# One turn in twelve units: first layers and sums grouped by three pairs in a graph layer on one core

## The chip, the core and the metric

The kernel runs on one core of a Trainium2 chip. The core has a matrix engine (TensorE, PE in the profile, with its weight loads as a row of their own, PEld), a vector engine (VectorE, DVE), a scalar engine (ScalarE, ACT), a general engine (GpSimd, POOL) and a queue engine (SyncE, SP). Each of them takes its own instructions in order, and they wait for one another by semaphores. Matrix results land in PSUM, which has eight banks of 2 KB a partition; everything else lies in SBUF. The metric is the time of one execution on the device, in microseconds (us). The time before is a median of 2561.25 us in three runs (2556.93 to 2567.58).

## The reference

One message-passing layer over 6250 nodes of 256 features and 206250 edges, sorted by target node. For every edge an embedding is made by three matrices, gated by a number of the edge, added to the row of the source node, clipped at zero, and summed by target; the sums go through a small network with a layer norm.

```python
h = relu(layernorm(x))
polarity = clip(edge_attr[:, 0:1], 0, 1);  raw = edge_attr[:, 1:]        # 64 features
e = relu(raw @ W_e1.T + b_e1) @ W_e2.T + b_e2
edge_emb = (e * (polarity + 0.01)) @ W_le.T + b_le
msg = relu(h[src] + edge_emb)
aggr = segment_sum(msg, dst)
t = (h + aggr) @ W_g1.T + b_g1
out = x + relu(layernorm(t) * ln_g + ln_b) @ W_g2.T + b_g2
```

All of it is in 32-bit floats. The kernel multiplies W_e2 and W_le together once, so that an edge needs two layers only. Each 32-bit matmul in the program stands as two matmuls in the profile.

## The kernel before

**Units, blocks and pairs.** The edges are cut into 806 units of 256 edges, two units to a block, two blocks to a pair: 202 pairs, four units each. Six blocks make a group, whose target nodes lie close together, so that its sums fit in 128 rows.

**The work of a unit.** `edge_part(u)` (L264 to L280) does the second layer: 8 matmuls in the profile (L272) into one PSUM bank, which DVE empties into a tile `msg` (L277). `gather` (L527) issues on POOL two gathers for the unit (L537), each bringing 128 rows of `hb_d` from memory into a tile `hg`. Some units later, `whole(u)` (L578) scales `msg` by the gate and adds it to the gathered rows on DVE (L584, two instructions), and ACT clips at zero (L589). How many units later is set by the loop: `LEAD - u // SHRINK`, from 22 units at the start down to 1 at the end.

**The work of a pair.** `first_layer(q)` (L238) makes the first layer of both blocks of a pair: 8 matmuls in the profile (L248) into four PSUM banks, three of which ACT empties (L257) and one DVE (L254). `add_pairs` (L622) sums the finished units of a pair by 16 matmuls in the profile (L601) with 0/1 matrices `sel`, into a bank of its own (`pd`). After the sums of a pair its `hg` tiles are free for later gathers. After the last block of a group `keep` (L606) copies the sums to SBUF on ACT (L613).

**Turns.** The first layers and the sums are issued together, in `turn_of(q)`, behind the second unit of a pair (`u % 4 == TURN`). In the first six and the last six pairs there is a turn in every pair: one first layer, the sums, one raw load. Between them (`by_two`) there is a turn in every second pair, so one in 8 units: the first layer of pair q+2, the sums of all pairs that are finished (two as a rule), the first layer of pair q+3, and two loads of raw features on SP (L235).

**What sets the order.** The instructions stand in the order in which the Python code issues them; no scheduler moves them. PSUM tiles `pz` rotate over seven banks, which second layers, first layers and node work share. In the main loop `forward(u)` comes first, then one small `piece()` of DVE work, then `whole` of the units that are due, then one step of node work (`due`). Two details belong to the turns: in the unit ahead of a turn one `whole` is held back (`made` is kept one lower), and no step of node work is issued in the unit ahead of a turn and in the turn (`now % 8 in QUIET`).

**Pacing of the gathers.** `in_step(us, behind)` (L546) is called behind each second layer, first layer and sum with an estimate of its PE time (1.754 us for a second layer, `EDGE`). It adds this to `spent` and issues gathers while `got * STEP < spent + AFLOAT` (1.282 us a gather, 6 us ahead), each batch behind the matmul named, and never more than the ring of `hg` tiles holds: `2 * (4 * summed + HG)`, with HG = 16 units. From unit 782 on, `gathers(4 * summed + HG)` issues without this pacing whatever the ring has room for.

Of the kernel before, what the change touches and what calls it, by code (L numbers as in the profile page):

```python
# [36 lines left out]
NP = -(-NB // 2)  # L37
MARGIN = 768
DEG = E // N
LEAD = 22  # L40
LEAST = 1
# [1 line left out]
STEP = 1.282  # L43
AFLOAT = 6.0
SHRINK = 36
HG = 16
FEW = 6
QUIET = (0, 1)
TURN = 1
CH = 4  # L50
AHEAD = 10
assert DEG * N == E and NF * GE + S * P >= E
# [21 lines left out]
def chunks():  # L74

    t = 0
    while t < NW:
        n = min(CH, N // P - t)
        if n <= 0:
# [17 lines left out]
def gnn_kernel(ctx: ExitStack, tc: tile.TileContext, x, src_c, dst_c, dst_r, pol_c, raw_t, w_e1t, w_e2,  # L97
               w_let, w_g1t, w_g2t, vec_c, row_v, x_t, out):
    nc = tc.nc
# [117 lines left out]
    with fast:  # L217
# [11 lines left out]
        def ps():  # L229
            return psz.tile([P, 2, D], F32, name="pz")  # L230

        def load_pair(q):
            if q < NP:
                raw[q] = ld.tile([P, 512], F32, name="raw")
                nc.sync.dma_start(out=raw[q], in_=raw_t[q])  # L235

        def first_layer(q):

            bs = [b for b in (2 * q, 2 * q + 1) if b < NB]
            if not bs:  # L240
                return
            for b in bs:
                e1[b] = e1_p.tile([P, 2, 512], F32, name="e1")
            pe = {}
            for c in range(2):
                for s, b in enumerate(bs):
                    pe[s, c] = ps().rearrange("p a b -> p (a b)")
                    z = nc.tensor.matmul(pe[s, c], we1_s[s * F:(s + 1) * F, c * P:(c + 1) * P],  # L248
                                         raw[q][s * F:(s + 1) * F, :], start=True, stop=True)
                paced(LAYER, z)  # L250
            for c in range(2):
                for s, b in enumerate(bs):
                    if s == c == 1:
                        nc.vector.tensor_scalar(e1[b][:, c, :], pe[s, c], be1_s[:, c:c + 1], 0.0, op0=ALU.add,  # L254
                                                op1=ALU.max)
                    else:
                        nc.scalar.activation(e1[b][:, c, :], pe[s, c], AF.Relu, bias=be1_s[:, c:c + 1])  # L257
            raw.pop(q)
# [5 lines left out]
        def edge_part(u):  # L264

            nonlocal last_z
            b, v = divmod(u, 2)
            pz = ps()
            for i in range(2):
                k = (2 * v + i) * P  # L270
                for c in range(2):
                    last_z = nc.tensor.matmul(pz[:, i, :], e1[b][:, c, k:k + P], wc_s[:, c, :], start=c == 0, stop=c == 1)  # L272
            msg[u] = msg_p.tile([P, 2, D], F32, name="msg")
            if plain(u):
                nc.scalar.activation(msg[u], pz, AF.Copy)
            else:
                nc.vector.tensor_add(msg[u], pz, bc_s)  # L277
            if v == 1:
                e1.pop(b)
            paced(EDGE, last_z)  # L280

        last_z = None
        sums = lambda last: None
        paced = lambda us, behind: None

        def by_two(q):
            return FEW <= q < NP - FEW

        def turn_of(q):


            if not by_two(q):
                if q + 2 < NP:
                    first_layer(q + 2)
                sums(q == NP - 1)
                load_pair(q + 4)
            elif q % 2 == 0:
                first_layer(q + 2)
                sums(False)
                first_layer(q + 3)  # L300
                load_pair(q + 4)
                load_pair(q + 5)

        def forward(u):

            edge_part(u)
            if u % 4 == TURN:
                turn_of(u // 4)
# [33 lines left out]
        with tc.tile_pool(name="p1", bufs=4) as p1, tc.tile_pool(name="p1x", bufs=11) as p1x:  # L342
# [4 lines left out]
            def load_rows(k, halves=1):  # L347
                if k < len(parts):
                    t0, p, t = parts[k]
                    xts[k] = p1x.tile([P, CH, D], F32, name="xt")  # L350
                    h = t // halves
# [4 lines left out]
            def stats(k, i0, i1):  # L356
                t0, p, t = parts[k]
                if i0 == 0:
                    mvs[k] = p1.tile([P, CH, 2], F32, name="mvx")
                for i in range(i0, min(i1, t)):  # L360
                    row_stats(p1, p, 1, lambda _: xts[k][:p, i, :], mvs[k][:, i:i + 1, :])

            def root(k):
                t0, p, t = parts[k]
                nc.scalar.activation(rs_s[:p, t0:t0 + t], mvs[k][:p, :t, 1], AF.Sqrt, bias=eps_t[:p])

            def nodes_out(k):
# [6 lines left out]
                for i in range(t):  # L374
                    nc.scalar.activation(xt[:p, i, :], xt[:p, i, :], AF.Relu, bias=nm_s[:p, t0 + i:t0 + i + 1],
                                         scale=rs_s[:p, t0 + i:t0 + i + 1])
                hb = p1.tile([P, CH, D], F32, name="hb")
                for i in range(t):
# [40 lines left out]
            for k in range(len(parts) + 1):  # L419
# [9 lines left out]
                if k < len(parts):  # L429
                    stats(k, 2, CH)  # L430
                    root(k)
# [3 lines left out]
                for _ in range((k > 0) + (k > 2 and k % 3 > 0)):  # L435
                    u = next(units, None)
# [84 lines left out]

        with tc.tile_pool(name="hg", bufs=HG) as hg_p, tc.tile_pool(name="ms", bufs=5) as ms_p, \
                tc.tile_pool(name="sel2", bufs=9) as sel2_p, tc.tile_pool(name="nd", bufs=3) as nd:
            got = 0
            acc = {}
            made = 0
# [17 lines left out]
            def gathers(last):  # L544

                while got < 2 * min(NU, last):  # L546
                    gather()

            def in_step(us, behind):

                nonlocal spent
                spent += us
                while got * STEP < spent + AFLOAT and got < 2 * min(NU, 4 * summed + HG):
                    gather(behind)
# [16 lines left out]
            def piece():  # L571

                if steps and steps[0][0] <= now:
                    steps.popleft()[1]()
                elif rest:
                    rest.popleft()[1]()
# [63 lines left out]
            now = 0  # L640
# [89 lines left out]
            def due():  # L730

                nonlocal spent
                fns = todo.pop(now, deque())
                if fns and not (by_two(now // 4) and now % 8 in QUIET):
                    spent += NODES
                    fns.popleft()()
                if fns:
                    todo.setdefault(now + 1, deque()).extendleft(reversed(fns))
# [11 lines left out]
            for u in range(LEAD, NU):  # L750
                now = u
                forward(u)

                if u >= NU - 24:
                    gathers(4 * summed + HG)

                piece()
                while made < u + 1 - max(LEAST, LEAD - u // SHRINK) - (by_two(u // 4) and (u + 1) % 8 == TURN):
                    gathers(made + 1)
                    whole(made)  # L760
                    made += 1
                due()
                if len(rest) > 6:
                    piece()
                if u == NU - 24:
                    for w in range(NW):
                        if groups_of(w)[-1] == NG - 1:
                            late[w] = node_work(w, True)
                if u == LEAD + 60:
                    flag = nc.values_load(bad_i[0:1, 0:1], min_val=0, max_val=3 * P)  # L770
            while todo:
                now = min(todo)
# [197 lines left out]
```

## Time and profile before

| | before |
|---|---|
| median of three runs | 2561.25 us (2556.93 to 2567.58) |
| the profiled execution | 2558.52 us, its span 2556.8 us |
| granted TensorE clock, mean | 0.965 |
| PE busy | 2378.9 us, 93% of the span |
| DVE / ACT / POOL busy | 1647.0 / 980.9 / 1638.7 us |
| second layers (L272) on PE | 1486.5 us busy, 51.8 us idle before |
| first layers (L248) on PE | 510.3 us busy, 42.8 us idle before |
| sums (L601) on PE | 258.6 us busy, 53.1 us idle before |
| gathers (L537) on POOL | 1612 of 993 ns |

The span is the time from the first to the last instruction on the core. PE's matmuls overlap and their ends are modelled, so a PE that is shown busy isn't always working at its full rate: the duration of a whole block of matmuls tells more than the busy share. In the chain of waits a row gives a start, a duration and what ran; in the groups a row gives line, engine, operation, tiles and count, then busy time and the mean of one, then the idle time of the engine just before and what ended it.

### The profile page before, as it was taken

The numbers are of one execution on the slowest core, as the hardware profiler recorded it, in microseconds if no ns is written. First come the engines' busy times: TensorE is split into PE (matmuls) and PEld (weight loads), VectorE is DVE, ScalarE is ACT, GpSimd is POOL, SyncE is SP. The second block draws the span as 40 slices with busy tenths as digits, with TensorE's granted clock in tenths as the row PEclk, the third lists the DMA queues.
The fourth block names the chain that finished last, engine by engine and source line by source line (L and its number), as shares of the span: only waits on it lengthen the run. The fifth ranks groups of instructions, "written<-read, shape, count | busy, mean of one in ns | idle before, by whom it ended". The sixth has DMA issues, their size and how long they took to land.

```text
span 2556.8 us, 35901 instructions
## 1 busy us (share of the span) xinstructions
PE 2378.9 (93%) x12382; PEld 1670.3 (65%) x12382; DVE 1647.0 (64%) x3953; ACT 980.9 (38%) x1701; POOL 1638.7 (64%) x1675
## 2 busy tenths in 40 slices
PE   9998998999999989999999999999999999899987
PEld 7666666666666757666666666666666666666664
DVE  7776666666666666666656666656666666656655
ACT  7333333343343433334333433433333433333432
POOL 5666666666666666666666666666666665666662
PEclk9999999999999999998999999999999999999998
DMA  8433343334334433433343444334334333343341
GB/s 300 129 115 113 108 134 112 114 114 130 113 108 125 130 119 106 133 108 117 111 144 101 115 126 122 110 106 137 112 114 131 118 107 114 109 131 109 119 119 55
DMA packets 156084, 309.24 MB, mean 121 GB/s; under 512 B 33183, under 2 KB 77944, under 8 KB 155896
## 3 DMA queue, kind: packets, MB, share of 16 engines
q0 software_dynamic: 77376, 211.39, 28.5%
q1 hardware_dynamic: 77364, 92.23, 11.4%
q10 hardware_dynamic: 1156, 3.28, 0.3%
q8 instruction: 98, 1.61, 0.3%
q14 instruction: 90, 0.74, 0.1%
HBM read 293.92 MB, written 12.85 MB: 120 GB/s over the span
## 4 chain that ended last, share of the span: by engine, by line
PE 82%; issue 5%; DVE 5%; another core or an unknown queue 3%; ACT 1%; DVEq 0%; ACTq 0%
PE pz L272 49%; PE pz L248 17%; PE pd L601 9%; PE pz L701 3%; DVE hg L584 2%; PE pz L195 2%; PE pz L169 2%; DVE msg L277 1%; ACT e L257 0%; DVE sel L566 0%; PE pz L185 0%; ACT hg L589 0%; DVE hT L676 0%; DVE e L254 0%
## 5 line engine op out<-in xcount | busy, mean ns | idle before, releaser
L537 POOL DMA_INDIRECT hg<-hb_d,src_s x1612 | 1601.5, 993 | 861.2 <-issue 525.4
L272 PE MATMUL pz<-wc_s,e 128*128 128x256 f32 x6448 | 1486.5, 384 | 51.8 <-issue 38.6
L272 PEld LDWEIGHTS pz<-wc_s,e 128*128 128x128 f32 x6448 | 1216.7, 192 | 318.8 <-issue 99.8
L589 ACT ACTIVATE hg<-hg 128x512 f32<-128x512 f32 x805 | 508.5, 632 | 1117.2 <-DVE hg L584 854.1
L277 DVE TENSOR_TENSOR msg<-pz,bc_s 128x512 f32<-128x512 f32 x799 | 546.6, 686 | 325.1 <-PE pz L272 152.3
L584 DVE SCALAR_TENSOR_TENSOR hg<-msg,pol_s,hg 128x256 f32<-128x256 f32 x1612 | 697.5, 480 | 2.6 <-issue 1.5
L248 PE MATMUL pz<-raw,we_s 64*128 64x512 f32 x1612 | 510.3, 653 | 42.8 <-issue 22.9
L254 DVE TENSOR_SCALAR e<-pz,vecs 128x512 f32<-128x512 f32 x201 | 150.5, 749 | 500.0 <-PE pz L248 201.4
L257 ACT ACTIVATE e<-pz,vecs 128x512 f32<-128x512 f32 x605 | 376.4, 686 | 225.1 <-PE pz L248 84.9
L248 PEld LDWEIGHTS pz<-raw,we_s 64*128 64x128 f32 x1612 | 177.2, 195 | 281.6 <-issue 164.7
L601 PE MATMUL pd<-hg,sel 128*32 128x256 f32 x3216 | 258.6, 408 | 53.1 <-issue 50.9
L601 PEld LDWEIGHTS pd<-hg,sel 128*32 128x32 f32 x3216 | 114.0, 115 | 221.2 <-issue 170.0
L566 DVE SCALAR_TENSOR_TENSOR sel<-iota_w,zero_c,rel 128x128 f32<-128x128 f32 x403 | 138.8, 344 | 0.0
L613 ACT ACTIVATE ms<-pd 128x256 f32<-128x256 f32 x66 | 25.5, 386 | 191.7 <-remote 60.1
L701 PEld LDWEIGHTS pz<-s,ms 128*128 128x128 f32 x548 | 70.3, 194 | 9.1 <-issue 3.8
L701 PE MATMUL pz<-s,ms 128*128 128x128 f32 x548 | 71.7, 278 | 4.7 <-issue 2.5
L676 DVE SCALAR_TENSOR_TENSOR hT<-hT,zero_c,stb 128x128 f32<-128x128 f32 (+1 forms) x196 | 67.2, 343 | 1.7 <-issue 1.7
L169 PE MATMUL pz<-wg_s,hT 128*128 128x256 f32 (+1 forms) x196 | 52.8, 389 | 9.9 <-DVE hT L703 7.4
L195 PE MATMUL pz<-wg_s,nT 128*128 128x256 f32 (+1 forms) x196 | 53.9, 393 | 5.6 <-ACT hg L589 2.7
L169 PEld LDWEIGHTS pz<-wg_s,hT 128*128 128x128 f32 (+1 forms) x196 | 36.5, 191 | 20.0 <-DVE hT L703 9.7
L379 POOL TENSOR_TENSOR hb<-xt,rows_b 128x256 f32<-128x256 f32 (+1 forms) x49 | 34.2, 729 | 23.4 <-DMA xt<-in_x_dram 12.7
L195 PEld LDWEIGHTS pz<-wg_s,nT 128*128 128x128 f32 (+1 forms) x196 | 37.7, 195 | 15.2 <-issue 6.4
(91 smaller groups left out, 393.0 us busy)
## 6 DMA issues: line engine op xcount, KB each, us to landing
raw<-in_raw_t_dram SPq DMA_DIRECT2D x202, 256.0 KB
hg<-hb_d,src_s POOLq DMA_INDIRECT x1612
stb<-st_d SPq DMA_DIRECT2D x49, 128.0 KB
hb_d<-hb SPq DMA_DIRECT2D x12, 512.0 KB
xt<-in_x_dram SPq DMA_DIRECT2D x48, 128.0 KB
hT<-in_x_t_dram SPq DMA_DIRECT2D x48, 128.0 KB
out_dram<-ot SPq DMA_DIRECT2D x48, 128.0 KB
xt<-in_x_dram SPq DMA_DIRECT2D x11, 512.0 KB
```

The lines of the kernel that those rows point to most:

```text
L169: nc.tensor.matmul(ph[:n, 0, :], aT[:, c, :n], wg1_s[:, c, :], start=c == 0 and not bias_by_pe, stop=c == 1)
L195: nc.tensor.matmul(po[:n, 0, :], nT[:, c, :n], wg2_s[:, c, :], start=c == 0, stop=c == 1)
L248: z = nc.tensor.matmul(pe[s, c], we1_s[s * F:(s + 1) * F, c * P:(c + 1) * P], raw[q][s * F:(s + 1) * F, :], start=True, stop=True)
L254: nc.vector.tensor_scalar(e1[b][:, c, :], pe[s, c], be1_s[:, c:c + 1], 0.0, op0=ALU.add, op1=ALU.max)
L257: nc.scalar.activation(e1[b][:, c, :], pe[s, c], AF.Relu, bias=be1_s[:, c:c + 1])
L272: last_z = nc.tensor.matmul(pz[:, i, :], e1[b][:, c, k:k + P], wc_s[:, c, :], start=c == 0, stop=c == 1)
L277: nc.vector.tensor_add(msg[u], pz, bc_s)
L537: g = nc.gpsimd.indirect_dma_start(out=hg[u][:, i, :], out_offset=None, in_=hb_d, in_offset=bass.IndirectOffsetOnAxis(ap=src_s[:, 2 * u + ...
L584: nc.vector.scalar_tensor_tensor(hg[u][:, i, :], m[:, i, :], pol_s[:, 2 * u + i:2 * u + i + 1], hg[u][:, i, :], op0=ALU.mult, op1=ALU.add)
L589: nc.scalar.activation(hg[u], hg[u], AF.Relu)
L601: z = nc.tensor.matmul(acc[g][j * W:(j + 1) * W, :], sel[g][:, k * S + j, :], m[:, j % 2, :], start=k == 0, stop=b == blocks_of(g)[-1])
L701: nc.tensor.matmul(pa[:, c, :n], ms[g][:, c * P:(c + 1) * P], box["sel2"][i][:, :n], start=i == 0, stop=i == len(gs) - 1)
```

## The change

Between the first six and the last six pairs there is now a turn in every third pair, one in 12 units: the first layer of pair q+1, the sums of all finished pairs (three as a rule), then the first layers of pairs q+2 and q+3 with nothing between them, and three raw loads. `at_turn(u)` names the turns, and the two details (one `whole` held back ahead of a turn, no node step in the turn and ahead of it) follow it. Since `hg` tiles are freed only by the sums, the ring grows from 16 to 20 units. [...]

```diff
-HG = 16
+HG = 20
 FEW = 6
-QUIET = (0, 1)
 TURN = 1
+SET = 3
...
-        def by_two(q):
+        def in_sets(q):
             return FEW <= q < NP - FEW
 
+        def at_turn(u):
+            q, v = divmod(u, 4)
+            return v == TURN and in_sets(q) and (q - FEW) % SET == 1
+
+        def layers_to(q):
+            nonlocal laid
+            while laid <= min(q, NP - 1):
+                first_layer(laid)
+                laid += 1
+
+        def loads_to(q):
+            nonlocal loaded
+            while loaded <= q:
+                load_pair(loaded)
+                loaded += 1
+
         def turn_of(q):
-            if not by_two(q):
-                if q + 2 < NP:
-                    first_layer(q + 2)
+            if not in_sets(q):
+                layers_to(q + 2)
                 sums(q == NP - 1)
-                load_pair(q + 4)
-            elif q % 2 == 0:
-                first_layer(q + 2)
+                loads_to(q + 4)
+            elif at_turn(4 * q + TURN):
+                layers_to(q + 1)
                 sums(False)
-                first_layer(q + 3)
-                load_pair(q + 4)
-                load_pair(q + 5)
+                layers_to(q + SET)
+                loads_to(q + 2 * SET)
+            elif q == FEW:
+                loads_to(q + SET + 1)
...
-                if fns and not (by_two(now // 4) and now % 8 in QUIET):
+                if fns and not (at_turn(now) or at_turn(now + 1)):
...
-                while made < u + 1 - max(LEAST, LEAD - u // SHRINK) - (by_two(u // 4) and (u + 1) % 8 == TURN):
+                while made < u + 1 - max(LEAST, LEAD - u // SHRINK) - at_turn(u + 1):
...
-    nc = bacc.Bacc("TRN2", target_bir_lowering=False, num_devices=1)
+    nc = bacc.Bacc("TRN2", target_bir_lowering=False, num_devices=1, dynamic_dma_scratch_size=8192)
```

1 line of the change is left out of this document (added).

## The prediction

> **What bounds the kernel now.** I read the page first, then the chain of waits over single turns, then the waits of PE, and last the timeline of POOL. On the page PE is busy nearly all the time, so the time is PE's, and three lines make up most of it.
>
> ```profile
> span 2556.8 us, 35901 instructions
> PE 2378.9 (93%) x12382; PEld 1670.3 (65%) x12382; DVE 1647.0 (64%) x3953; ACT 980.9 (38%) x1701; POOL 1638.7 (64%) x1675
> ...
> L537 POOL DMA_INDIRECT hg<-hb_d,src_s x1612 | 1601.5, 993 | 861.2 <-issue 525.4
> L272 PE MATMUL pz<-wc_s,e 128*128 128x256 f32 x6448 | 1486.5, 384 | 51.8 <-issue 38.6
> ...
> L584 DVE SCALAR_TENSOR_TENSOR hg<-msg,pol_s,hg 128x256 f32<-128x256 f32 x1612 | 697.5, 480 | 2.6 <-issue 1.5
> L248 PE MATMUL pz<-raw,we_s 64*128 64x512 f32 x1612 | 510.3, 653 | 42.8 <-issue 22.9
> ...
> L257 ACT ACTIVATE e<-pz,vecs 128x512 f32<-128x512 f32 x605 | 376.4, 686 | 225.1 <-PE pz L248 84.9
> ...
> L601 PE MATMUL pd<-hg,sel 128*32 128x256 f32 x3216 | 258.6, 408 | 53.1 <-issue 50.9
> ```
>
> The chain shows what these cost when nothing disturbs them: first a stretch of second layers and a turn of two pairs, then sums of three pairs, which already occur here and there.
>
> ```profile
> 1198.26 5.18 PE pz L272 x24
> 1203.44 1.92 PE pz L248 x8
> 1205.36 1.86 PE pd L601 x32
> 1207.22 1.92 PE pz L248 x8
> 1209.14 3.65 PE pz L272 x16
> ```
>
> ```profile
> 2163.93 2.73 PE pd L601 x48
> 2166.66 1.92 PE pz L248 x8
> ```
>
> A first layer is 1.92 us, the sums of two pairs 1.86 us, of three 2.73 us: 0.87 us a pair and 0.12 us for the switch. A second-layer matmul in a stretch takes 5.18 / 24 = 0.216 us; 16 of them behind a turn take 3.65 us, 0.20 us over 16 x 0.216.
>
> Now compare with the groups. First layers take 510.3 + 42.8 = 553 us for 202 pairs, clean they would be 202 x 1.92 = 388: 165 us over. Sums take 258.6 + 53.1 = 312 us, clean 202 x 0.87 + 101 x 0.12 = 188: 124 us over. So about 289 us, 2.9 us in each of some 101 turns, are lost in turns; second layers lose little, with 51.8 us idle. What these 289 us are decides the case. The view of line L248 names, for one part, who ended the wait (us, times):
>
> ```profile
>   DVE msg L277: 75.7, 103
>   DVE hg L584: 22.0, 50
>   DVE e L254: 15.0, 22
> ```
>
> Some 113 us of waiting of first layers for DVE: PSUM banks that DVE hasn't emptied yet. The other part, some 176 us, is named "issue". It looks like this (columns of the last fence: stretch, its length, busy us and count of PE, PEld, DVE, ACT and POOL, clock, DMA):
>
> ```profile
> 952.70 0.36 issue
> 953.07 0.38 PE pd L601
> 953.44 1.08 issue
> 954.52 0.59 PE pd L601 x2
> 955.11 0.82 issue
> 955.94 0.38 PE pd L601
> ```
>
> ```profile
> 1203.30:1209.20 5.90, 5.90 (x50) 2.44 (x50) 1.83 (x4) 3.02 (x6) 2.91 (x4) 1.00 0.22 67
> 951.10:960.20 9.10, 4.68 (x35) 1.86 (x33) 3.45 (x8) 2.70 (x4) 5.55 (x6) 0.81 0.34 101
> ```
>
> In the clean turn PE does first layer, sums and first layer in 5.9 us, and POOL issues 4 gathers with a pause. In the slow one the sums alone take 9.1 us: PE gets one matmul about every 0.7 us, while POOL issues gather after gather (here 6). The largest such place is near the end:
>
> ```profile
> 2480.58 0.95 POOL L537 DMA_INDIRECT hg<-hb_d,src_s  x1 [0.30 <-issue]
> ...
> 2499.38 0.95 POOL L537 DMA_INDIRECT hg<-hb_d,src_s  x1 [0.30 <-issue]
> 2508.29 0.95 POOL L537 DMA_INDIRECT hg<-hb_d,src_s  x1 [7.96 <-ACT e L257]
> ```
>
> ```profile
> 2489.70 0.69 DVE L277 TENSOR_TENSOR msg<-pz,bc_s 128x512 f32<-128x512 f32 x1 [8.21 <-remote]
> 2502.36 0.69 DVE L277 TENSOR_TENSOR msg<-pz,bc_s 128x512 f32<-128x512 f32 x1 [10.91 <-remote]
> ```
>
> From 2480.58 to 2499.38 POOL issues 16 gathers, 1.25 us apart, without a pause (the batch that unit 785 issues unpaced). In that time DVE stands still for 8.21 and 10.91 us with no releaser known, and moves on 2 us after the last gather's end. So I read "issue" as what a long unbroken run of gathers does to the other engines. Why it does, the trace doesn't say.
>
> [...]
>
> **The change part by part.**
>
> *Switches between kinds of matmul.* In the pairs 6 to 195 there were 95 turns, now 63. Two first layers in a row occur in the trace:
>
> ```profile
> 72.74 3.87 PE L248 MATMUL pz<-raw,we_s 64*128 64x512 f32 x16
> 76.54 0.70 PE L272 MATMUL pz<-wc_s,e 128*128 128x256 f32 x2
> ```
>
> From start to start 3.80 us, and not held up by the seven banks. Six pairs before: 3 x (1.92 + 1.86 + 1.92 + 0.20) = 17.70 us. After: 2 x (1.92 + 2.73 + 3.80 + 0.20) = 17.30 us. That is 0.40 us in six pairs, and 190 / 6 x 0.40 = **12.7 us less**. No matmul goes away; this is PE's own time and lies on the path wherever the turn is clean.
>
> *Stalls in turns.* 95 of the turns at 2.9 us are 275 us. With 63 turns and a stall f times as long each, they are 183 f. If a turn keeps its stall (f = 1), that is 92 us less. If the stall follows the work in a turn (f = 1.5), nothing changes. If the longer stretch makes it worse, f = 1.8 (the upper end I allow, midway between the mean of 2.9 us and the excess of the slow turn above, 9.1 - 1.86 = 7.2 us) adds 54 us. I take it by parts. The 176 us go with gathers, whose number doesn't change, so 1.5. The 113 us for banks lie between: DVE's backlog builds up over 12 units and not over 8, but the two first layers at the end now come 0.87 us later behind the first one, and node steps are spread over 10 of 12 units and not 6 of 8, so 1.25. The mean is (176 x 1.5 + 113 x 1.25) / 289 = 1.40: **19 us less**.
>
> *The ring.* Room left just ahead of the sums is what it was: 20 - 12 is 16 - 8. Pacing is by PE time, so the ring binds more rarely. At unit 785 it costs: the sums there free the ring, the unpaced line fills it at once, and its reach is four units longer, so the batch is 24 gathers for 16. With DVE stopped as in the rows above, 8 more at 1.25 us are **10 us more**. Bounds: 0, if the longer stop only moves the others' work, and 20 if the stop grows faster than the run.
>
> [...]
>
> *At nothing.* Three raw loads in a turn for two: the number of loads is the same, and the third waits on SP until the first layer of q+2 has read its tile, some 6.6 us into the turn. Behind it on SP stand node loads and stores, and what these bring is used at least three units later, 3 x 1.73 us and the rest of the turn; if that cover went, DVE would wait in `ready`. On ACT the three evictions of a first layer (0.69 us each) fit within the next one's 1.9 us. The held-back `whole` (2 x 0.48 us on DVE) and the quiet units become rarer by a third, worth nothing while DVE waits for PE in turns.
>
> [...]
>
> [...]
>
> The sum: -12.7 - 19 + 10 = about -22 us. The profiled execution took 2558.5 us, 2.7 us below the median. The new median is then 2561 - 22 = **2539 us**, 0.9% less.
>
> **Rivals.**
>
> *The stall belongs to the turn.* f = 1 to 1.2: each turn loses its 2.9 us, however much it holds. For it: DVE's backlog is limited by the seven banks, so it can't grow by half. Against: the slow issue. Time at f = 1.1: -12.7 - 74 + 10, 2484 us.
>
> *Slower: runs of gathers go unbroken.* In a stretch of second layers PE releases 1.754 / 1.282 = 1.37 gathers a unit, 1.71 us of POOL in 1.73 us of PE, so POOL hardly pauses; it is turns that break the run, and they come every 24 gathers, not 16. If runs are stopped by the freeze and not by a turn, DVE, PE and then the clock (0.81 in the slow turn above) pay each time. At f = 1.8: -12.7 + 54 + 10, 2612 us. From f = 1.52 on it is slower than before. [...]
>
> *Nothing is won.* The gathers alone are 1612 x 1.25 = 2015 us of POOL, so whatever PE saves packs them closer and comes back as freezes: f = 1.5, 2558 us.
>
> **How the numbers follow.** About 0.5%, 12.8 us, can be told from no change. My forecast (f from 1.25 to 1.5) has 0.42, the stall of the turn 0.14, unbroken runs 0.32, nothing won 0.12. The first is faster by over 12.8 us for f below 1.45, three quarters of it: 0.31, and with the second 0.45 for faster. The rest of the first and most of the fourth is 0.20 for same; 0.35 for slower. The forecast's own range is 2515 to 2560 us. The range takes half of the second (f = 1.1) and the slower case up to f = 1.75: 2485 to 2603 us.
>
> **What would show it.** Right: in the chain, clean turns of 1.92, 2.73 and 3.80 us; L601's idle and busy sum near 300 us, L248's near 520; DVE's waits before L248 below 100 us in all; a stop of DVE near the end that is 10 us longer, with 24 gathers in a run from unit 785 on. Wrong: L272 with over 100 us idle (freezes have moved into the stretches), L248 waiting over 130 us for DVE, a granted clock below 0.955, or gathers over 1.1 us on POOL.

## The result, and the profile after

The changed kernel takes **2595.23 us** (median of 4 runs, 2590.02 to 2598.06), the kernel before beside it 2559.09 us (4 runs). The ratio is **1.0143, interval 1.0117 to 1.0169**: 1.4% slower, where 0.9% faster was forecast. The profiled execution took 2598.06 us, 39.5 us more than that of before.

These are the rows of the page of after that answer to those shown of before. The sums are now line L620, the gathers L556.

```profile
span 2596.3 us, 35351 instructions
PE 2394.4 (92%) x12382; PEld 1702.0 (66%) x12382; DVE 1656.9 (64%) x3953; ACT 977.7 (38%) x1701; POOL 1623.4 (63%) x1675
...
L556 POOL DMA_INDIRECT hg<-hb_d,src_s x1612 | 1586.1, 984 | 906.7 <-issue 539.3
L272 PE MATMUL pz<-wc_s,e 128*128 128x256 f32 x6448 | 1472.1, 385 | 10.0 <-issue 8.5
...
L248 PE MATMUL pz<-raw,we_s 64*128 64x512 f32 x1612 | 492.0, 667 | 62.3 <-ACT e L257 31.7
...
L620 PE MATMUL pd<-hg,sel 128*32 128x256 f32 x3216 | 307.0, 402 | 113.5 <-issue 105.7
```

Adding busy and idle time line by line says roughly where the 39.5 us came from (the rows of different lines overlap a little). Sums went from 311.7 to 420.5 us: +108.8. First layers stayed, 553.1 and 554.3. Second layers fell from 1538.3 to 1482.1: -56.2. The three lines of node matmuls (L701 before, L169, L195) fell by 19.3 together. The sum of these is +34.5. So the stretches got cleaner and the turns much worse.

The view of line L248, which the prediction used, says who ended the waits (us, times):

```profile
  issue: 247.7, 602
  ACT e L257: 81.9, 40
  DVE msg L277: 17.5, 35
  DVE hg L603: 10.8, 34
```

In this view waiting for DVE has gone from 113 us to 29. But it adds up the idle time of two rows, the matmuls (PE) and their weight loads (PEld), which run beside the matmuls. The waits of PE alone are much smaller (who waited, for whom: us, times, longest), first of before, then of after:

```profile
PE pz L248 <- DVE msg L277: 15.2, 15, 3.8
PE pz L248 <- DVE hg L584: 1.3, 1, 1.3
```

```profile
PE pz L248 <- ACT e L257: 31.7, 16, 7.4
PE pz L248 <- DVE msg L277: 2.3, 4, 0.7
```

So PE itself waited 16.5 us for DVE ahead of first layers, not 113, and 2.3 us after the change. What grew is "issue" ahead of the sums (50.9 to 105.7 us, in the pages) and the wait for ACT's evictions. A typical turn in the chain (start, length, what):

```profile
1229.81 2.06 PE pz L248 x8
1231.87 1.84 PE pd L620 x27
1233.71 0.30 issue
1234.01 0.42 PE pd L620 x2
1234.43 1.03 issue
...
1236.79 1.50 issue
1238.30 1.54 PE pd L620 x16
1239.84 4.85 PE pz L248 x16
1244.68 3.65 PE pz L272 x16
```

The sums begin at full pace, 27 matmuls in 1.84 us, and then come one or two at a time. They take 7.97 us for a clean 2.73, and the two first layers behind them 4.85 for 3.80 (3.63 in e6 and e14).

Those two first layers don't wait in the chain; they run at a lower clock. Two stretches right behind a stop, the first from before (one first layer behind the slow turn shown in the prediction), the second the one above (columns as there: stretch, length, busy us and count of PE, PEld, DVE, ACT and POOL, clock, DMA):

```profile
960.19:963.82 3.63, 3.63 (x9) 1.72 (x8) 0.00 (x0) 1.74 (x4) 1.90 (x2) 0.54 0.13 36
1239.84:1244.68 4.84, 4.84 (x17) 1.94 (x17) 0.75 (x1) 3.05 (x6) 3.62 (x5) 0.75 0.41 124
```

In the first a first layer takes 3.63 us at a granted clock of 0.54; in the clean turn of the prediction it took 1.92 us at 1.00. So a stop costs more than the time for which PE stands still.

### The profile page after: what moved, and what is told of

The parts are those of the page before. It is cut to its first block, busy times and chain, and to the rows that moved or that the text cites. A ratio compares the mean times of both kernels' runs of the same rounds, so it can differ in the third digit from the quotient of the medians.

```text
span 2596.3 us, 35351 instructions
## 1 busy us (share of the span) xinstructions
PE 2394.4 (92%) x12382; PEld 1702.0 (66%) x12382; DVE 1656.9 (64%) x3953; ACT 977.7 (38%) x1701; POOL 1623.4 (63%) x1675
## 4 chain that ended last, share of the span: by engine, by line
PE 85%; issue 7%; DVE 3%; ACT 2%; another core or an unknown queue 1%; POOL 1%; DMA 1%; ACTq 0%; POOLq 0%; DVEq 0%
PE pz L272 51%; PE pz L248 17%; PE pd L620 11%; PE pz L720 2%; PE pz L169 2%; PE pz L195 2%; ACT e L257 1%; DVE hg L603 1%; POOL hg L556 1%; DVE msg L277 1%; PE pz L185 0%; DMA xt<-in_x_dram 0%; DMA hg<-hb_d,src_s 0%; ACT hg L608 0%
## 5 line engine op out<-in xcount | busy, mean ns | idle before, releaser
L556 POOL DMA_INDIRECT hg<-hb_d,src_s x1612 | 1586.1, 984 | 906.7 <-issue 539.3
L272 PEld LDWEIGHTS pz<-wc_s,e 128*128 128x128 f32 x6448 | 1229.5, 193 | 237.1 <-ACT e L257 47.1
L248 PE MATMUL pz<-raw,we_s 64*128 64x512 f32 x1612 | 492.0, 667 | 62.3 <-ACT e L257 31.7
L257 ACT ACTIVATE e<-pz,vecs 128x512 f32<-128x512 f32 x605 | 370.4, 690 | 124.5 <-PE pz L248 67.2
L620 PE MATMUL pd<-hg,sel 128*32 128x256 f32 x3216 | 307.0, 402 | 113.5 <-issue 105.7
L248 PEld LDWEIGHTS pz<-raw,we_s 64*128 64x128 f32 x1612 | 181.7, 206 | 312.5 <-issue 224.3
L620 PEld LDWEIGHTS pd<-hg,sel 128*32 128x32 f32 x3216 | 129.1, 112 | 302.0 <-issue 245.4
L169 PE MATMUL pz<-wg_s,hT 128*128 128x256 f32 (+1 forms) x196 | 52.1, 387 | 5.3 <-issue 2.2
L195 PE MATMUL pz<-wg_s,nT 128*128 128x256 f32 (+1 forms) x196 | 50.5, 380 | 0.8 <-ACT nT L188 0.8
L169 PEld LDWEIGHTS pz<-wg_s,hT 128*128 128x128 f32 (+1 forms) x196 | 37.3, 192 | 12.6 <-issue 2.9
L195 PEld LDWEIGHTS pz<-wg_s,nT 128*128 128x128 f32 (+1 forms) x196 | 37.0, 190 | 6.4 <-ACT nT L188 1.4
```

Source lines behind the costliest of these rows:

```text
L169: nc.tensor.matmul(ph[:n, 0, :], aT[:, c, :n], wg1_s[:, c, :], start=c == 0 and not bias_by_pe, stop=c == 1)
L195: nc.tensor.matmul(po[:n, 0, :], nT[:, c, :n], wg2_s[:, c, :], start=c == 0, stop=c == 1)
L556: g = nc.gpsimd.indirect_dma_start(out=hg[u][:, i, :], out_offset=None, in_=hb_d, in_offset=bass.IndirectOffsetOnAxis(ap=src_s[:, 2 * u + ...
L620: z = nc.tensor.matmul(acc[g][j * W:(j + 1) * W, :], sel[g][:, k * S + j, :], m[:, j % 2, :], start=k == 0, stop=b == blocks_of(g)[-1])
```

## The experiments

I use one measure throughout. The **excess** is the busy and idle sums of first layers and sums together, less what they take clean: 388 us for first layers, 0.87 us a pair and 0.12 us a burst for the sums (184 us in the changed kernel, 188 before, 200 with a burst in every pair). It is 289 us before and 403 us after. The column beside it is the busy and idle sum of second layers. Ratios are to the kernel before, run beside each kernel in its batch; its median was 2559 us beside the changed kernel, 2524 to 2529 us in the next four batches and 2179 us in the last (more on that below). Two things limit the comparison. The ranges expected of e1, e2, e3 and e5 count from 2561 us, and their batch ran at 2526, so I go by ratios. And e3, with the same turns as the kernel before, has 237 us of excess where that has 289: across batches, differences of some 50 us in this column say little.

| kernel | median us | ratio (interval) | excess us | second layers us |
|---|---|---|---|---|
| before (profile of before) | 2559.1 | 1 | 289 | 1538 |
| changed | 2595.2 | 1.0143 (1.0117 to 1.0169) | 403 | 1482 |
| e1_split_sums | 2548.5 | 1.0091 (1.0069 to 1.0113) | 352 | 1484 |
| e2_no_gathers_in_turn | 2900.3 | 1.1499 (1.1477 to 1.1521) | 301 | 1821 |
| e3_ring_only | 2522.0 | 0.9997 (0.9975 to 1.0018) | 237 | 1542 |
| e5_before_split | 2533.4 | 1.0029 (1.0009 to 1.0048) | 263 | 1541 |
| e6_rows_plain | 2157.6 | 0.8533 (0.8487 to 0.8579) | 2 | 1448 |
| e7_before_rows_plain | 2170.3 | 0.8583 (0.8537 to 0.8629) | 20 | 1452 |
| e8_rows_half_plain | 2168.7 | 0.8576 (0.8530 to 0.8623) | 9 | 1449 |
| e9_afloat2 | 2556.7 | 1.0121 (1.0072 to 1.0170) | 359 | 1472 |
| e10_loads_later | 2570.9 | 1.0161 (1.0119 to 1.0203) | 372 | 1495 |
| e14_quiet_turn | 2967.8, one run | - | 117 | 2106 |
| e4_turn_every_pair | 2504.8 | 0.9910 (0.9874 to 0.9945) | 164 | 1602 |
| e13_sums_apart | 2516.6 | 0.9957 (0.9937 to 0.9977) | 134 | 1644 |
| e16_every_pair_afloat2 | 2502.0 | 0.9896 (0.9869 to 0.9922) | 134 | 1619 |
| e15_few_sums | 2535.3 | 1.0044 (1.0017 to 1.0071) | 287 | 1534 |
| e17_more_signals (last batch) | 2179.6 | 1.0001 (0.9990 to 1.0011) | 27 | 1453 |
| e18_fewer_signals (last batch) | 2175.7 | 0.9985 (0.9976 to 0.9995) | 14 | 1446 |
| e20_every_pair_fewer (last batch) | 2208.6 | 1.0132 (1.0115 to 1.0148) | 27 | 1480 |
| e21_more_signals_plain (last batch) | 2170.5 | 0.9956 (0.9940 to 0.9972) | 20 | 1453 |

### Burst, gathers in the turn, or ring?

**e1**: the sums in three bursts.

```diff
-                layers_to(q + 1)
-                sums(False)
-                layers_to(q + SET)
+                for k in range(1, SET + 1):
+                    layers_to(q + k)
+                    sums(False, 1 if k < SET else NP)
...
```

> The changed kernel, but with the sums of one pair (16 matmuls) behind each of the turn's three first layers in place of 48 matmuls in one burst; gathers, ring and turns as in the changed kernel. Clean it costs 0.24 us a turn more for two more switches, 15 us in all. Theory A (a burst of sums longer than some 25 to 45 matmuls runs PE's instructions dry, and each then comes 0.7 us after the last): the stall goes with the bursts; the sums' busy and idle sum falls from 420 us to below 300, the time to 2400 to 2500 us. Theory B (gathers that POOL issues in the turn hold PE up): as many gathers fall into the turn as before, so the stall stays; 2590 to 2620 us.

Neither. In its batch the changed kernel would take 2525.81 x 1.0143 = 2562 us, so splitting wins 13 us. Of 403 us of excess, 352 are left, with bursts of 16 matmuls. 77.6 us of that is a wait that the edit let in (26 times, sums wait for ACT's eviction of a finished group, which now stands inside the turn). Each takes 3.0 us on the mean for an eviction of 0.38 us, so the same stall may be in it. Theory A as stated falls. That PE ran out of instructions isn't borne out by the trace of the changed kernel either: it has 183 DMA packets of the kind "instruction", which I take for the fetches of instructions, and none starts between those at 1217.07 and 1244.46, while the stop shown above begins and ends in between.

**e2**: no gather released within the turn.

```diff
+                held = True
                 layers_to(q + 1)
                 sums(False)
                 layers_to(q + SET)
+                held = False
...
-                while got * STEP < spent + AFLOAT and got ...
+                while not held and got * STEP < spent + AFLOAT and got ...
```

> The changed kernel, but no gather is released by the steps of the turn; what falls due there is issued behind the next second layers. The burst of 48 sums stays. Theory A: the burst alone does it, the sums keep some 420 us, 2585 to 2615 us. Theory B: the turn is clean (1.92, 2.73, 3.80 us), the sums take below 300 us, and the time is 2400 to 2500 us.

Both missed, by some 300 us and more. Second layers rose by 339 us: the gathers that were held back fall due behind the turn, and the stall went there (PE waited 197.7 us for "issue" ahead of second layers, for 8.5 in the changed kernel). By my estimate it also didn't do what it was built for: `AFLOAT` lets POOL have 6 us of gathers released ahead of the turn, and it would still work on them in it. e14, below, holds them earlier.

**e3**: the ring and `dynamic_dma_scratch_size=8192` alone. The setting is what the expectation calls the halved descriptor area; that it halves one, no run shows.

```diff
-HG = 16
+HG = 20
...
-num_devices=1)
+num_devices=1, dynamic_dma_scratch_size=8192)
```

> The kernel before with the ring of 20 units and the halved descriptor area alone; the turns are as before. Theory C (the ring or the halved area makes the loss): 2585 to 2600 us. Theories A and B, where the turns make it: 2555 to 2575 us, 10 us of it for the batch of 24 gathers at unit 785.

No change within 0.25%: theory C falls, and the 10 us that I gave the batch at unit 785 are not there either. (In its trace the gathers there come as runs of 20 and 16, not as a longer one.)

**e5**: the kernel before, split in the same way.

```diff
                 first_layer(q + 2)
-                sums(False)
+                sums(False, 1)
                 first_layer(q + 3)
+                sums(False)
...
```

> The kernel before, but with the sums of one pair (16 matmuls) behind each of the turn's two first layers in place of 32 in one burst. Clean it costs 0.12 us a turn, 11 us in all. Theory A: most bursts of 32 were clean already, so it wins what the others lost, up to 100 us: 2460 to 2540 us. Theory B: the gathers in the turn are as many, 2555 to 2580 us.

7.6 us slower, about what one more burst in each turn costs (11 us clean). In microseconds that lies in theory A's range, but only because the batch as a whole was faster; as a ratio of 1.0029 it wins nothing, and theory A falls here too.

### Are the gathers the cause at all?

**e6, e7, e8**: all gathers, or every second, replaced by plain loads of as many bytes. They bring neighbouring rows in place of the indexed ones, so the output isn't the reference's, and only the time counts.

```diff
-                g = nc.gpsimd.indirect_dma_start(
-                    out=hg[u][:, i, :], out_offset=None, in_=hb_d,
-                    in_offset=bass.IndirectOffsetOnAxis(ap=src_s[:, 2 * u + i:2 * u + i + 1], axis=0))
+                r = (got * P) % (N - P)
+                g = nc.sync.dma_start(out=hg[u][:, i, :], in_=hb_d[r:r + P, :])
```

> The changed kernel, but its 1612 gathers of rows by index on POOL are plain loads of 128 neighbouring rows each, on SP's queue: the same bytes into the same tiles at the same places in the program, with POOL almost idle; the sums then add up the wrong rows, so only the time counts. Theory G (POOL's gathers make every stall: while POOL issues them without a pause, the other engines' instructions and signals come late): the stalls vanish, the sums' busy and idle sum falls from 420 us to 190 to 230 us, the first layers' from 554 to 390 to 450 us, the time to 2250 to 2400 us. Theory A (the burst of 48 sums runs PE's instructions dry by itself): the sums keep over 350 us, 2500 to 2600 us.

> The kernel before with the same edit, plain loads on SP's queue in place of the gathers. Theory G: 2260 to 2410 us, and some 10 to 15 us above the changed kernel with plain loads, which is what its fewer switches are worth once nothing stalls. Theory A: 2480 to 2560 us, and below the changed kernel with plain loads.

> The changed kernel, but of each unit's two gathers only the first is made by POOL and the second is a plain load on SP's queue, so POOL has half as many and has to pause. Theory G: a run of gathers breaks off before it does harm, so well over half of the gain of the kernel with plain loads alone, 2280 to 2430 us. Theory A: 2500 to 2600 us.

Page rows of e6, then of e8:

```profile
PE 2141.6 (99%) x12382; PEld 1617.7 (75%) x12382; DVE 1650.7 (77%) x3953; ACT 978.7 (45%) x1701; POOL 37.2 (2%) x63
...
L248 PE MATMUL pz<-raw,we_s 64*128 64x512 f32 x1612 | 386.1, 608 | 0.0
L619 PE MATMUL pd<-hg,sel 128*32 128x256 f32 x3216 | 187.8, 381 | 0.0
```

```profile
L557 POOL DMA_INDIRECT hg<-hb_d,src_s x806 | 798.3, 990 | 1261.0 <-ACT hg L612 377.2
...
L624 PE MATMUL pd<-hg,sel 128*32 128x256 f32 x3216 | 188.7, 382 | 0.0
```

PE is 99% busy, and the sums take 187.8 us without a wait. Both kernels gained more than I expected (2250 us and up). With half of the gathers left on POOL the stall is gone as well. It isn't the amount of DMA traffic: e6 moves the same 309 MB in less time (143 GB/s on the mean for 119 in the changed kernel). And once nothing stalls, the change is worth 2170.27 - 2157.62 = **12.65 us** (two runs of each; those of e6 lie 2.5 us apart). So in this batch the gathers on POOL were behind the stalls, in turns and elsewhere: 358 us before (2528.7 - 2170.3), and about 407 us in the changed kernel (2528.7 x 1.0143 - 2157.6).

### What in the gathers?

**e9**: the lead of POOL cut.

```diff
-AFLOAT = 6.0
+AFLOAT = 2.0
```

> The changed kernel, but POOL may run ahead of PE by 2 us of gathers in place of 6. A stall in a turn then makes POOL wait for PE earlier. Theory G: the stalls end sooner, the sums' busy and idle sum falls below 350 us, 2500 to 2570 us. Theory A: within 15 us of the changed kernel; later gathers may cost some, up to 2630 us.

The sums fell from 420.5 to 373.3 us, but the time stayed within the interval of the changed kernel's. The lead has some effect, not the one expected. The time of 2556.7 us lies in the ranges of both theories, so the run doesn't decide between them.

**e10**: raw loads five units behind the turn.

```diff
                 layers_to(q + SET)
-                loads_to(q + 2 * SET)
...
+            if u >= 5 and at_turn(u - 5):
+                loads_to((u - 5) // 4 + 2 * SET)
```

> The changed kernel, but the three raw loads of a turn are issued five units behind it, in the stretch, and not while the turn runs. Theory R (it is the raw load together with the gathers that holds PE up; 21 of 96 slow places in the changed kernel begin 2 to 3 us after a raw load was issued): the turn's excess of 5.6 us falls below 3 us, 2450 to 2520 us. Theory G without it (gathers alone): within 15 us of the changed kernel, 2545 to 2580 us.

1.0161 (1.0119 to 1.0203) against 1.0143: the raw loads have no part in it that can be told here, and theory R, with 2450 to 2520 us, falls.

**e14**: POOL quiet in the turn.

```diff
-                while got * STEP < spent + AFLOAT and got ...
+                while not any(at_turn(now + k) for k in range(4)) and got * STEP < spent + AFLOAT and got ...
```

> The changed kernel, but no gather is released from three units ahead of a turn to its end, so that POOL has worked off its lead of 6 us and stands still in the turn; 12 to 14 gathers then follow at once. Theory G: the turn is clean (sums' busy and idle sum 190 to 240 us, first layers 390 to 430 us), and the stalls come in the stretch behind it, from the tenth or so gather of the long run on; the time is no better, 2600 to 2900 us. Theory A: the sums keep over 350 us.

The timeline of POOL (start, length, operation; in brackets the idle time ahead of it and what ended it), then the chain, over one turn and the stretch behind it:

```profile
1223.92 0.94 POOL L556 DMA_INDIRECT hg<-hb_d,src_s  x1 [0.30 <-issue]
1234.95 0.94 POOL L556 DMA_INDIRECT hg<-hb_d,src_s  x1 [10.08 <-ACT hg L608]
...
1255.03 0.95 POOL L556 DMA_INDIRECT hg<-hb_d,src_s  x1 [0.30 <-issue]
1259.21 0.95 POOL L556 DMA_INDIRECT hg<-hb_d,src_s  x1 [3.23 <-remote]
```

```profile
1224.00 1.92 PE pz L248 x8
1225.92 2.73 PE pd L620 x48
1228.65 3.63 PE pz L248 x16
...
1243.41 7.12 PE pz L272 x33
1250.53 1.43 issue
...
```

With POOL still, the burst of 48 sums takes 2.73 us. Then 17 gathers run without a pause from 1234.95 to 1255.98. PE works at full pace until 1250.53, which is after 12 of them, and then gets almost nothing until some 2 us behind the last. In this turn and the stretch behind it the reading of the prediction holds, and over the whole run the excess fell from 403 to 117 us. But second layers rose by 623 us, since the gathers have to be made up for. The one run there is missed theory G's numbers on the high side (sums 267 us for 190 to 240, 2968 us for 2600 to 2900); theory A, with sums over 350 us, falls.

The stop here comes 15.6 us after the run of gathers began. In the turn of after shown in the result it came sooner. The run that it belongs to begins ahead of the turn and goes on without a pause to 1236.37:

```profile
1225.27 0.94 POOL L556 DMA_INDIRECT hg<-hb_d,src_s  x1 [1.77 <-PE pz L272]
```

From there to the stop at 1233.71 are 8.4 us. By the matmuls that PE started in that time the two are nearer than by time, 76 in e14 and 56 in the turn, where 27 of them are sums. That would let a dense turn reach the stop sooner than a stretch does. It is a comparison of single places, and not a proof.

### What in the turn?

**e4**: a turn in every pair. **e13**: in addition the sums two units behind the first layer.

```diff
         def by_two(q):
-            return FEW <= q < NP - FEW
+            return False
```

```diff
-                sums(q == NP - 1)
+                if q < FEW or q >= NP - FEW:
+                    sums(q == NP - 1)
...
+            if u % 4 == 3 and FEW <= u // 4 < NP - FEW:
+                sums(False)
```

> The kernel before, but with a turn in every pair (first layer of one pair, sums of one pair) all the way, twice as many turns with half as much in each. Clean it costs 0.54 us for each two pairs, 51 us. If the stall grows faster than what a turn holds (one pair below 1 us, two pairs 2.7 us, three pairs 5.6 us a turn), the stalls fall by 80 to 150 us: 2440 to 2500 us on this chip, below the kernel before. If it grows in step with it (1.3 us a turn): 2560 to 2590 us.

> The kernel before with a turn in every pair, and the sums two units behind the first layer, so that sixteen second-layer matmuls lie between them. Clean it costs some 0.8 us for each two pairs, 75 us. If what counts is how much dense work follows without a stretch between, the stalls in turns almost go: 2440 to 2520 us. If the stall is paid for each place where the kind of matmul changes: 2600 to 2680 us.

e4 is 0.9% faster than the kernel before although its clean cost was put 51 us higher (e20, its relative, measures 29.5 us where nothing stalls). Its 2505 us lie just above the first range. e13 is 0.4% faster, for a clean cost put at 75 us, and lies in its first range. Divide the excess by 202 pairs: 0.66 us in e13, 0.81 in e4, 1.17 in e3 (turns of two pairs), 2.0 in the changed kernel (1.43 in the profile of before, which is of the changed kernel's batch). The stall grows faster than what a turn holds. In return second layers are longer the smaller the turn: 1644, 1602, 1542, 1482 us, for 1448 to 1452 in e6 and e7. So part of the stall has moved there.

**e15**: half as many sums.

```diff
+                few = g < NG - 1 and 0 < k < L - 1 and b > 2 * FEW and b < NB - 2 * FEW
...
                 for j in range(S):
+                    if few and j:
+                        break
```

> The changed kernel with half of the sums left out (of a group's six blocks the inner four keep one matmul of four), so a turn holds 24 matmuls of sums in the trace in place of 48 and is 1.4 us shorter; gathers, first layers and pacing are as they were, and the output lacks those rows. Clean it saves 66 x 1.4 = 92 us. Theory D (gathers alone don't stop PE, but a run of gathers stops it the sooner, the more instructions PE issues in that time, so the dense sums decide): the turn's excess falls from 5.6 us to 2 to 3.5 us, 2290 to 2400 us. If only the length of the turn and the gathers in it count: the excess stays at 4.5 to 5.6 us, 2420 to 2490 us.

The timeline, PE first, then ACT, DVE and POOL:

```profile
1208.02 2.78 PE L623 MATMUL pd<-hg,sel 128*32 128x256 f32 x24
1210.72 3.70 PE L248 MATMUL pz<-raw,we_s 64*128 64x512 f32 x14
1219.69 2.07 PE L248 MATMUL pz<-raw,we_s 64*128 64x512 f32 x2 [5.28 <-ACT e L257]
...
1218.68 0.38 ACT L635 ACTIVATE ms<-pd 128x256 f32<-128x256 f32 x1 [7.83 <-remote]
...
1218.85 0.75 DVE L254 TENSOR_SCALAR e<-pz,vecs 128x512 f32<-128x512 f32 x1 [8.98 <-remote]
...
1215.76 0.95 POOL L556 DMA_INDIRECT hg<-hb_d,src_s  x1 [0.30 <-issue]
1219.00 0.95 POOL L556 DMA_INDIRECT hg<-hb_d,src_s  x1 [2.29 <-remote]
```

The expectation was built on a turn 1.4 us shorter, and that is wrong: 24 such sums take 2.78 us, as long as 48 did, so clean there is nothing to save. For the rest the run meets neither range and doesn't tell the theories apart: the excess falls from 403 to 287 us, second layers rise by 52, and the ratio of 1.0044 is 1.0 points below the changed kernel's. The rows show something else. The sums are clean, and the stall stands behind them. The sums end at 1210.80, and ACT's eviction of them, the next on its list, begins at 1218.68. DVE's eviction of a bank that PE wrote meanwhile begins at 1218.85. PE goes on alone until seven banks are full (the 14 matmuls of the row, two a bank). ACT, DVE and POOL move again within 0.4 us, 2.0 us behind the end of the last gather in the run (1216.71). I read this as finished work of PE that the others didn't hear of. In this view the turn is the worst place for it, since there each matmul group of a first layer needs an eviction, four a pair in 1.9 us, where a stretch needs one in 1.73 us.

**e16**: e4 with the lead cut to 2 us.

> The kernel with a turn in every pair, which was faster than the kernel before, and in it POOL may run ahead of PE by 2 us of gathers in place of 6. If a stall lasts for as long as POOL has gathers released, it ends sooner: 2460 to 2500 us, 1 to 2% below the kernel before. If the lead doesn't matter: 2500 to 2510 us.

0.9896 against 0.9910 of e4, intervals overlapping: the lead matters little. Of the kernels that compute the reference, e16 and e4 are the fastest in the batches that stall, ahead of both kernels of this case.

### Signals, and a batch without stalls

**e17** adds four signals of PE to each turn; **e21** is e17 with plain loads; **e18** (on the changed kernel) and **e20** (on e4) take signals away.

```diff
+                    mid_z = z if j == 1 else mid_z
+                if 2 * FEW < b < NB - 2 * FEW:
+                    a = nc.vector.memset(seen[0:1, :], 0.0)
+                    tc.add_manual_dep(a.ins, mid_z.ins.name, ...)
```

```diff
-                paced(SUMS, z)
+                paced(SUMS, last_f)
```

> The kernel before, with four more signals from PE in each turn and no other work: behind the second matmul of each block's sums DVE clears one number, which nobody reads, once that matmul is done. Theory S (what a gather run holds up is PE's signals to the other engines, which then get out at some 0.5 to 0.6 per us; a stretch sends 0.58 per us, one per unit, and keeps up, a turn sends some 10 in 6 us, the changed kernel's 15 in 8.5 us): the stall per turn grows from 2.7 us to 5 us or more, 2650 to 3000 us. Theory T (the stall belongs to the time that a turn takes, whatever PE signals): 2515 to 2560 us.

> The control: the kernel before with plain loads for gathers and the same four more signals in each turn. Both theories: they cost next to nothing without gathers, 2168 to 2190 us against 2170 us.

> The changed kernel, but the gathers that the sums release wait for the first layer ahead of the sums and not for the sums, so PE sends one signal less in each turn of some 15. Theory S: up to 1.8 us a turn, 2440 to 2540 us on this chip. Theory T: within 15 us of the changed kernel, 2545 to 2580 us.

> The kernel with a turn in every pair, with the same edit: 123 signals less, 0.65 in each turn. Theory S: up to 1.1 us a turn, 2350 to 2490 us, the fastest that computes the reference. Theory T: 2495 to 2515 us.

The question stayed open, for a reason that neither theory had: in this batch nothing stalled. The kernel before itself took 2179.09 us (20 runs, 2177.87 to 2181.38), 14% less than in the batches ahead of it, with not a line changed. e21 (2170.50 us) equals e7 (2170.27), so the signals cost nothing by themselves. Rows of the page and of the chain of e17:

```profile
PE 2164.5 (99%) x12382; PEld 1606.0 (74%) x12382; DVE 1677.8 (77%) x4331; ACT 981.9 (45%) x1701; POOL 1632.9 (75%) x1675
...
L538 POOL DMA_INDIRECT hg<-hb_d,src_s x1612 | 1595.6, 990 | 499.1 <-issue 333.9
...
L603 PE MATMUL pd<-hg,sel 128*32 128x256 f32 x3216 | 194.3, 382 | 0.0
```

```profile
1206.08 1.92 PE pz L248 x8
1208.00 1.86 PE pd L603 x32
1209.86 1.92 PE pz L248 x8
1211.78 3.65 PE pz L272 x16
```

POOL idles 499.1 us ahead of 1612 gathers, 0.31 us each: it issues them almost without a pause from start to end. A gather takes 990 ns, as before. And PE is 99% busy. So long runs of gathers are not enough for a stall; something else has to be there, which was present in five batches and not in the sixth, and which no view of the traces names. It isn't tied to one chip as far as the record goes: the batch of e1, e2, e3 and e5, which stalled, and the last one carry the same chip number, 8. Nor did the transfers of the gathers change: their packets took 28.5% of the DMA engines' time in 2557 us before and 33.5% in 2177 us here, 729 us both times. Where nothing stalls, the gathers cost 9 us (2179.1 against 2170.5 in e21). The changed kernel itself was not run in this batch. With the edit of e18 it is 3.4 us faster than the kernel before, and e20, the relative of the winner e4, is 1.3% slower.

## Why the prediction was wrong, step by step

**Switches (-12.7 us): right, with luck in the last digits.** With plain loads on both sides the difference is 12.65 us. But the clean turn, in e14, is 1.92, 2.73 and 3.63 us, so two first layers in a row take 3.63 us and not 3.80. With that the sum of the prediction gives 0.74 us in six pairs, 23 us. First layers and sums together are indeed 22.6 us shorter in e6 than in e7 (573.9 for 596.5); other lines gave part of it back.

**Stalls in turns (-19 us): the step that failed.** I had put f, the stall of a turn of three pairs over one of two, at 1.40 and at most 1.8. Measured: 403 us of excess, 14 of them outside the turns as before, so 389 / 183 = 2.1. That is +114 us in place of -19. (The 14 are taken over from the prediction's own sum and not measured. With the 20 and 2 us that e7 and e6 have without stalls taken off, the growth is 132 us.) The wrong reasoning is the sentence "the 176 us go with gathers, whose number doesn't change, so 1.5". That gathers are behind the stall is shown by e6 to e8; but the stall doesn't go with their number. It goes with where PE is while they run: little in a stretch of the changed kernel, and 0.66, 0.81, 1.17 and 2.0 us a pair as the turn grows. (The four values are from three batches.) Why it grows so is open.

The part for banks (113 us, f of 1.25) rested on a misreading: the view adds the idle time of the weight loads to that of the matmuls. PE itself waited 16.5 us for DVE there before and 2.3 us after, so the 289 us were never 113 of one kind and 176 of another. ACT's evictions, which the prediction put at nothing, cost 31.7 us of PE's waiting in their place; e6, without the stall, has no such wait.

**What I left out: the stretches.** Second layers won 56 us and node matmuls 19 us; the prediction gave them no term. With plain loads second layers win only 4 us (1452 to 1448), so most of that is stall that isn't there any more, and that 114 us more in the turns made only 39.5 us in all is due to it.

**The ring (+10 us): its premise was wrong.** The run has the 24 gathers forecast, but it had 24 before as well. The prediction counted 16 from 2480.58 on, and the run without a pause had begun eight gathers earlier. So nothing got longer: DVE's stops are 6.04 and 12.21 us, 18.3 together, for 19.1 before. The timeline, the run's first gather of before, then POOL and DVE of after (start, length, engine and operation; in brackets the idle time ahead of it and what ended it):

```profile
2469.36 1.14 POOL L537 DMA_INDIRECT hg<-hb_d,src_s  x1 [2.56 <-ACT hg L589]
```

```profile
2503.60 0.94 POOL L556 DMA_INDIRECT hg<-hb_d,src_s  x1 [5.07 <-issue]
...
2532.54 0.94 POOL L556 DMA_INDIRECT hg<-hb_d,src_s  x1 [0.30 <-issue]
...
2524.94 0.42 DVE L197 TENSOR_TENSOR ot<-pz,xt 128x256 f32<-128x256 f32 x1 [6.04 <-remote]
2537.58 0.69 DVE L277 TENSOR_TENSOR msg<-pz,bc_s 128x512 f32<-128x512 f32 x1 [12.21 <-remote]
```

e3 measures the ring at 0.9997.

**At nothing: right but for ACT's evictions above.** The raw loads (e10, 1.0161 against 1.0143) and the setting `dynamic_dma_scratch_size=8192` (e3, 0.9997; gathers of 984 ns in the changed kernel, of 993 before) cost nothing that can be measured.

**The rivals.** "Slower" had the sign, and the time of 2595 us lies between its 2558 and 2612. Its mechanism exists: in e14 a run of 17 gathers stops PE in the stretch, 15.6 us after it began. But it isn't what happened in the changed kernel, whose second layers idle 10.0 us, far from the 100 us that would have spoken for it. "The stall belongs to the turn" (f up to 1.2) and "nothing is won" (f = 1.5) are refuted by f = 2.1. Of the signs set down beforehand, DVE's waits below 100 us came true and spoke for nothing; of those for "wrong", a granted clock below 0.955 came true, barely (0.954); the sums at 420.5 us (300 forecast) and first layers at 554.3 us (520) decided.

**Without the stall term.** In the last batch PE is 99% busy beside 1612 gathers (e17), and in e6 it is 99% busy beside as many bytes of plain loads. In the other batches PE and ACT did stand still, and that was tied to the gathers on POOL. Without the stall term and the ring, the sum would have come out at -12.7 us.

**Open.** What it is that makes gathers hold up PE in one batch and not in another. And why the stall grows faster than the turn: its sums in one burst (e1), the raw loads (e10) and the ring (e3) don't explain it; that it is the number of PE's signals in a turn is a guess, and the runs meant to test it met no stall. Whether it goes by the number of matmuls since the gathers' run began is untested too. And every run on record has a span and a granted clock, so as far as the record shows all were recorded as they ran; whether the recording has a part in the stall can't be told from them.

## What to carry to other kernels

Before a stall's cost is scaled to a new schedule, ask what the stalled engine was doing in it: a cause that is spread evenly (gathers all the time) can still be charged almost wholly to one kind of place, and then the cost goes with the size of that place and not with the cause. Take the cause away altogether, as the plain loads did: that gives the value of the change where nothing stalls (12.65 us) and the size of what the cause costs (358 us). And before a wait is made a term of a sum, see whose wait it is: idle time of weight loads that run beside the matmuls isn't time of PE. And a few per cent won against a disturbance hold only while it is there: the order that won 0.9% here lost 1.3% where nothing stalled (with the small edit of e20).

## What the runs showed of the hardware that was not expected

- The same program takes 2524 to 2559 us in five batches of runs and 2179 us in a sixth, at a granted clock of 0.97 and 0.998. For the same 12382 matmuls PE is busy 2378.9 us (idle 178) in the profile of before and 2164.5 us (idle 12) in that of e17; gathers take as long in both (993 and 990 ns).
- Where it stalls, a run of gathers leaves PE alone at first (15.6 us, 12 gathers, 76 matmuls in e14; 8.4 us, 6 gathers, 56 matmuls in the turn of after) and then all but stops it until some 2 us behind the run's end (4.1 us in the run of 24 near the end of after).
- Behind such a stop the granted clock was lower: 0.54 in a first layer that took 3.63 us in place of 1.92.
- In such a stop PE can go on while ACT and DVE don't take up work that PE has finished (7.83 and 8.98 us in e15), and ACT, DVE and POOL resume within 0.4 us of one another.
- 24 sums in groups of one matmul take as long (2.78 us) as 48 in groups of four (2.73 us).
